# Running counts of the experts' choices: sums of neighbours and of pairs in fixed tiles, in place of a row of additions

## The chip, the cores and the metric

The kernel runs on one core of a Trainium2 chip. A core has five engines that run side by side and wait for each other through semaphores: TensorE (PE, matrix products; its weight loads are shown apart as PEld), VectorE (DVE), ScalarE (ACT), GpSimd (POOL) and SyncE (SP, which here only issues DMAs). The metric is the device time of one execution in microseconds (us), the median over several runs. The kernel before takes 1328.57 us (three runs, 1328.46 to 1329.15).

## The reference

The input x holds 8192 tokens of 512 numbers. Each token is normalized (layernorm), and the output is x plus two terms of the normalized tokens: a random-feature attention (exponentials of projections, times a matrix of weights) and a mixture of 64 experts with a shared expert beside them. The part that the change touches is the routing of the mixture:

```python
scores = sigmoid(tokens @ router_w)              # 8192 x 64
# the 4 best of 8 groups of experts are kept, and of these the 8 best experts
topk_w, topk_idx = top_k(masked_scores, 8)
flat_e = topk_idx.reshape(-1)
onehot = one_hot(flat_e, 64)
prior = cumsum(onehot, axis=0) - onehot          # choices of that expert by earlier tokens
pos = take_along_axis(prior, flat_e[:, None], axis=1)[:, 0]
valid = pos < 256                                # an expert takes its first 256 choices
```

So every expert serves the first 256 tokens that chose it, and the kernel needs, for every expert, the running count of choices over the tokens.

## The kernel before

**Stages.** The tokens are worked on in 16 blocks of 512. A block is four chunks of 128 tokens; inside a tile the 128 partitions are the tokens of a chunk, and the four chunks (index s, NS = 4) lie side by side in the columns. Until about 395 us the kernel runs a loop over the even blocks (function `dense`: shared expert `ps_gu`, features `ps_f`, the sums `ps_o`), and `routing` steps a generator `look_up(b)` for every block, even and odd, between the steps of `dense`. From there on it finds the chosen tokens of each expert (`seek`, gathers on POOL's queue), and runs the 64 experts (`hidden`, `down`), with the attention of the odd blocks laid between them (`late_attention`), and the shared expert of the odd blocks at the end (`ends`).

**One block in `look_up`.** PE transposes the normalized tokens (`ps_x`, line 356; from block 5 on they come as the copy `xc`, which POOL's queue makes by a DMA, line 339), ACT and DVE split each of the four results into a high part (line 99) and a low part `xT_l` (line 102). PE forms the logits `ps_l` (line 398), ACT copies them to `lt`, PE turns them back (`ps_lt`, line 415), and DVE works out the penalty of the groups (lines 431 to 448), the eight best of each chunk (`max`, `match_replace`, lines 459 and 460) and from these `mask_r` (line 462): 1 where a token chose an expert. `mask_r` has 128 partitions and 4 x 64 columns.

**The running sums.** `prior_r[:, s, :]` shall hold, for each partition, how often earlier chunks chose each expert. It starts with a copy of `taken`, the total of all earlier blocks (line 467). Three additions of 64 columns follow, each of which needs the one before it (line 469), and a fourth makes the new `taken` (line 472). PE then adds over the partitions: the product `both`/`ps_bu` of `prior_r` with a matrix of ones (line 479), and four small products of `mask_r` with a triangle and of `prior_r` with ones (line 490). ACT copies one half to `cu` and SP stores it (`upto`, lines 498 and 499); DVE adds from the other half to `begun` (line 518). After the last block, `chunks` turns `begun` into the lines that POOL gathers (lines 753 to 756).

**What sets the order.** The program is written in an order of yields, and a scheduler places each engine's instructions by their priorities and by an estimate of when operands are ready; `behind(a, b)` adds an edge that keeps a after b on an engine. In the code such edges hold the counting product behind the last product of the dense stream (line 486). Each engine then runs its own list strictly in order.

**Pools.** `ps_sm` holds two banks of PSUM, used in turn for two of the four transposes of a block, for `ps_l`, `ps_lt` and `ps_bu`. In the odd blocks `ps_bu` takes the bank of the second transpose, and `ps_l` of the following block that of the fourth: each is free when its `xT_l` is done. `rt` holds `mask_r`, `prior_r` and `j` once each; `act` has four slots of 2 KiB with the tag "t"; `const` is allocated for the whole run.

Of the kernel before, what the change touches and what calls it, by code (L numbers as in the profile page):

```python
# [9 lines left out]
FP = mybir.dt.float32  # L10
FPR = mybir.dt.float32r
I32 = mybir.dt.int32
AF = mybir.ActivationFunctionType
ALU = mybir.AluOpType
# [4 lines left out]
P = 128  # L19
# [3 lines left out]
E = 64  # L23
# [10 lines left out]
NS = TB // P  # L34
# [14 lines left out]
TAKEN = -3.0e38  # L49
# [5 lines left out]
def rfs_attention_moe_kernel(  # L55
# [15 lines left out]
    nc = tc.nc  # L71
    xf = x.flatten_outer_dims()

    const = ctx.enter_context(tc.tile_pool(name="const", bufs=1))
# [7 lines left out]
    rt = ctx.enter_context(tc.tile_pool(name="rt", bufs=1))  # L82
    act = ctx.enter_context(tc.tile_pool(name="act", bufs=4))
# [159 lines left out]
    nc.gpsimd.iota(erow_i, pattern=[[1, E]], base=-E, channel_multiplier=0)  # L243
    erow = const.tile([P, E], FP, name="erow")
    nc.gpsimd.tensor_copy(erow, erow_i)
    taken = const.tile([P, E], FP, name="taken")
    nc.vector.memset(taken, 0.0)

    begun = [const.tile([P, NS, E], FP, name=f"begun{h}") for h in range(NH)]
    for t in begun:  # L250
# [126 lines left out]
    def look_up(b):  # L377
# [78 lines left out]
        mr = gt_t  # L456
        top = rt.tile([P, NS, K], FP, tag="top", name="top", bufs=2)
        for s in range(NS):
            nc.vector.max(top[:, s, :], ml[:, s, :])
            nc.vector.match_replace(mr[:, s, :], top[:, s, :], ml[:, s, :], TAKEN)  # L460
        mask_r = rt.tile([P, NS, E], FPR, tag="mask", name="mask_r")
        nc.vector.tensor_scalar(mask_r, mr, TAKEN * 0.9, None, ALU.is_le)
        mask = mask_r.bitcast(FP)

        prior_r = rt.tile([P, NS, E], FPR, tag="prior", name="prior_r")
        prior = prior_r.bitcast(FP)
        nc.vector.tensor_copy(prior_r[:, 0, :], taken)
        for s in range(1, NS):
            nc.vector.tensor_tensor(
                prior_r[:, s, :], prior[:, s - 1, :], mask[:, s - 1, :], ALU.add  # L470
            )
        nc.vector.tensor_tensor(taken, prior[:, NS - 1, :], mask[:, NS - 1, :], ALU.add)
        yield
        yield

# [190 lines left out]
    for rc in range(RC):  # L666
        pool, tag = ((ps_sm, "sm"), (ps_tr, "tr"))[rc // 2]
# [52 lines left out]
    normed[0] = normalize(0, *scale0)  # L720
    split0 = last["split"]
    late = look_up(0)
    next(late)
    upper0 = last["upper"]
# [25 lines left out]
    def chunks():  # L750

        for h in range(NH):
            j = rt.tile([P, E], FP, tag="j", name="j")
            nc.vector.tensor_reduce(j, begun[h].rearrange("p s e -> p e s"), AX.X, ALU.add)
            nc.vector.scalar_tensor_tensor(line[:, :, h], j, float(E), erow, ALU.mult, ALU.add)
            nc.vector.tensor_scalar(first_of[:, :, h], j, float(P), -float(P), ALU.mult, ALU.add)
# [28 lines left out]
    def seek():  # L785

        chunks()
        ats = {}
        for e in range(E + TE):
            n, k = divmod(e, TE)  # L790
            if e < E:
                if k == 0:
                    ats[n] = kib4([P, TE, NH, P], "at", FP)
                find(ats[n], e)
            if k == 1 and n:
                tokens_of(n - 1, ats.pop(n - 1), last["dve"])
            yield
# [114 lines left out]
    def routing(t):  # L912

        for b in sorted(fronts):
            if next(fronts[b], fronts) is fronts:
                del fronts[b]
        b, k = divmod(t + GAP, GAP)
        if k == (b == 1) and b < NB:
            fronts[b] = look_up(b)
            next(fronts[b])  # L920
        if k == GAP - 3 and b + 1 < NB:
            normed[b + 1] = normalize(b + 1, *roots(b + 1, statistics(xbs[b + 1])))
        if k == 1 and b + 2 < NB:
            xbs[b + 2] = load_tokens(b + 2)
# [144 lines left out]
```

## Time and profile before

| what | value |
|---|---|
| median of the timed runs | 1328.57 us (1328.46 to 1329.15) |
| the profiled execution, its own time | 1306.77 us |
| its span, first to last instruction | 1304.9 us |
| granted TensorE clock | 1.00 |
| PE idle in the first 400 us | 4.56 us, of which 2.49 us before 40 us |
| PE idle between 400 and 1200 us | 0.56 us |
| PE idle after 1200 us | 5.55 us |

The profile takes one execution, and it is 1.9 us longer than its span; the timed runs are 21.8 us longer than the profiled one. Busy times of an engine are summed over its instructions where they don't overlap. Matmuls are pipelined: a matmul's record is longer than the distance to the next one's start (here 0.39 us against 0.226 us for 512 columns), and so the waits of PE are read from the starts. The same holds of DVE: the record of an addition over 64 columns has 0.22 us, and the next instruction starts 0.13 us after it.

### The profile page before, as it was taken

To read this page: it belongs to the slowest core of one execution; us is meant where nothing else is said; L and a number is where in the kernel's file an instruction comes from. 1 tells how busy PE (TensorE), PEld (TensorE's weight loads), DVE (VectorE), ACT (ScalarE), POOL (GpSimd) and SP (SyncE) were. 2 spreads that over 40 slices of the span, in tenths; PEclk is the share of its full clock that TensorE was granted. 3 is DMA by queue.
4 is the path that set the end of the run, shared out by engine and by line. 5 is a ranking of instruction groups with operands and counts; after the bars stand their busy time and mean duration, and the time that the engine had idled before them with its cause. 6 is when DMAs were issued, how large, how long until landed. Compare 5 with 4: busy or idle time off the path is not lost.

```text
span 1304.9 us, 21429 instructions
## 1 busy us (share of the span) xinstructions
PE 1294.3 (99%) x7670; PEld 1136.6 (87%) x7670; DVE 922.3 (71%) x1911; ACT 646.6 (50%) x1025; POOL 587.3 (45%) x690
## 2 busy tenths in 40 slices
PE   9999999999999999999999999999999999999998
PEld 7888888888888989999999999999999999988886
DVE  6978867867865776777767677777776776643555
ACT  5744444453432655566566465665665665540111
POOL 3122122113107666777677767667667654310000
PEclk9999999999999999999999999999999999999999
DMA  8665675676586989999999999999999999784995
GB/s 271 227 234 199 243 281 213 219 282 235 190 297 190 320 221 334 251 292 285 299 283 261 272 284 276 256 316 279 283 261 296 283 257 249 195 245 166 317 320 193
DMA packets 189530, 338.61 MB, mean 259 GB/s; under 512 B 15984, under 2 KB 87664, under 8 KB 189424
## 3 DMA queue, kind: packets, MB, share of 16 engines
q1 hardware_dynamic: 153488, 245.93, 54.7%
q0 software_dynamic: 35936, 91.32, 29.7%
q8 instruction: 60, 0.98, 0.3%
q14 instruction: 46, 0.38, 0.1%
HBM read 220.66 MB, written 104.99 MB: 250 GB/s over the span
## 4 chain that ended last, share of the span: by engine, by line
PE 85%; DVE 8%; DMA 2%; ACT 2%; issue 1%; SPq 1%; POOL 1%; ACTq 0%; DVEq 0%; POOLq 0%
PE ps_gu L109 41%; PE ps_e L109 13%; PE ps_o L109 10%; PE ps_y L109 6%; PE ps_fu L109 5%; PE ps_t L832 3%; PE ps_f L109 3%; PE ps_l L398 2%; DMA xb<-in_L_attn_x_dram 1%; DVE f L527 1%; PE ps_x L356 1%; DVE xT_l L102 1%; DVE st L300 1%; SPq L287 1%; POOL at L762 1%
## 5 line engine op out<-in xcount | busy, mean ns | idle before, releaser
L890 POOL DMA_INDIRECT out_dram<-ye,who x128 | 229.3, 1792 | 180.5 <-ACT ye L889 120.1
L109 PE MATMUL ps_gu<-gT,gu_h 128*128 128x256 f32 x2048 | 292.3, 285 | 0.0
L109 PEld LDWEIGHTS ps_gu<-gT,gu_h 128*128 128x128 f32 x2048 | 265.2, 190 | 9.0 <-ACT gu_h L99 4.7
L762 POOL DMA_INDIRECT at<-upto,line x128 | 139.3, 1088 | 76.0 <-DMA q<-norms 37.3
L102 DVE TENSOR_TENSOR gu_l<-gu,gu_h 128x1024 fp32r<-128x1024 f32 x128 | 155.3, 1223 | 14.6 <-ACT gu_h L99 13.7
L109 PE MATMUL ps_gu<-gT,gu_l 128*128 128x256 f32 x1024 | 164.7, 283 | 0.0
L815 POOL DMA_INDIRECT xg<-xnw,who x128 | 138.8, 1084 | 40.0 <-issue 32.0
L109 PE MATMUL ps_e<-d_h,ehT 128*128 128x512 f32 x512 | 147.8, 390 | 0.0
L109 PEld LDWEIGHTS ps_gu<-gT,gu_l 128*128 128x128 f32 x1024 | 142.6, 191 | 3.4 <-DVE gu_l L102 0.6
L99 ACT CAST gu_h<-gu 128x1024 fp32r<-128x1024 f32 x128 | 132.2, 1047 | 0.0
L889 ACT ACTIVATE ye<-ps_e,we 128x512 f32<-128x512 f32 x128 | 87.6, 688 | 84.6 <-PE ps_e L109 84.3
L109 PEld LDWEIGHTS ps_e<-d_h,ehT 128*128 128x128 f32 x512 | 94.7, 188 | 18.8 <-ACT d_h L99 0.2
L271 POOL TENSOR_TENSOR a<-rstd,ve 128x4 f32<-128x4 f32 x45 | 10.9, 243 | 201.5 <-DVE rstd L262 199.0
L99 ACT CAST ehT<-sg 128x512 fp32r<-128x512 f32 x64 | 39.9, 623 | 124.5 <-DVE sg L535 113.3
L535 DVE SCALAR_TENSOR_TENSOR sg<-sg,ps_gu 128x512 f32<-128x512 f32 x64 | 44.0, 687 | 71.4 <-PE ps_gu L109 71.4
L102 DVE TENSOR_TENSOR gT<-ps_t,gT 128x512 fp32r<-128x512 f32 x128 | 82.1, 683 | 16.8 <-ACT gT L99 16.8
L102 DVE TENSOR_TENSOR d_l<-d,d_h 128x1024 fp32r<-128x1024 f32 x64 | 78.2, 1222 | 11.7 <-ACT d_h L99 11.7
L541 ACT ACTIVATE f<-f,ab 128x512 f32<-128x512 f32 x64 | 46.3, 724 | 73.4 <-DVE f L527 72.7
L109 PE MATMUL ps_o<-wT_h,fT 128*128 128x512 f32 x288 | 80.1, 391 | 0.2 <-ACT fT L99 0.2
L109 PE MATMUL ps_e<-d_l,ehT 128*128 128x512 f32 x256 | 79.2, 390 | 0.0
L109 PE MATMUL ps_o<-d_h,hT 128*128 128x512 f32 x256 | 79.0, 396 | 0.0
L533 ACT ACTIVATE sg<-ps_gu 128x512 f32<-128x512 f32 x64 | 38.3, 598 | 77.3 <-PE ps_gu L109 77.3
(181 smaller groups left out, 2523.6 us busy)
## 6 DMA issues: line engine op xcount, KB each, us to landing
gu<-in_L_ffn_gate_w_dram SPq DMA_DIRECT2D x64, 512.0 KB
gu<-in_L_ffn_up_w_dram SPq DMA_DIRECT2D x64, 512.0 KB
d<-in_L_ffn_down_w_dram SPq DMA_DIRECT2D x64, 512.0 KB
xnw<-xw SPq DMA_DIRECT2D x32, 577.0 KB
xb<-in_L_attn_x_dram SPq DMA_DIRECT2D x32, 512.0 KB
out_dram<-xb SPq DMA_DIRECT2D x32, 512.0 KB
xT_h<-turned SPq DMA_DIRECT2D x30, 512.0 KB
xT_l<-turned SPq DMA_DIRECT2D x30, 512.0 KB
```

The costliest lines, as they stand in the source:

```text
L99: return nc.scalar.copy(dst, src)
L102: return on.tensor_tensor(dst, src, hi.bitcast(FP), ALU.subtract)
L109: last["pe"] = nc.tensor.matmul(ps, w[c][a], v[c][b], start=(start and part == 0 and c == 0), stop=(stop and part == 2 and c == n - 1),)
L398: logits = nc.tensor.matmul(pl, rwp[:, kc].rearrange("p t e -> p (t e)"), v[kc], start=(n == 0 and kc == 0), stop=(n == 1 and kc == KC - 1),)
L533: last["tanh"] = nc.scalar.activation(dst, g, AF.Tanh, scale=0.5)
L535: nc.vector.scalar_tensor_tensor(dst, dst, 0.5, u, ALU.mult, ALU.mult)
L541: nc.scalar.activation(f, f, AF.Exp, scale=ab[:, rc : rc + 1])
L762: nc.gpsimd.indirect_dma_start(out=at[:, e % TE, h, :], out_offset=None, in_=upto, in_offset=bass.IndirectOffsetOnAxis(ap=line[:, e, h : h ...
L815: nc.gpsimd.indirect_dma_start(out=xgs[e][:, h, :], out_offset=None, in_=xnw, in_offset=bass.IndirectOffsetOnAxis(ap=who[:, e, h : h + 1], ...
L832: turned_s = nc.tensor.transpose(pr[:, c, ts(h, P)], xr[:, h, ts(c2 * 2 + c, P)], ident_r)
L889: nc.scalar.activation(ye[:, h, :], po, AF.Copy, scale=wes[e][:, h : h + 1])
L890: now = nc.gpsimd.indirect_dma_start(out=out, out_offset=bass.IndirectOffsetOnAxis(ap=who[:, e, h : h + 1], axis=0), in_=ye[:, h, :], in_o ...
```

## The change

The three additions in a row are replaced by two. Two tiles, `masks` and `sums`, each with five slots of 64 columns, are allocated once for the run. Slot 0 of `masks` holds what earlier blocks chose (the old `taken`), slots 1 to 4 the masks of the four chunks. The first addition puts the sum of each slot and its left neighbour into `sums[1..4]` (256 columns). The second adds to `sums[2..3]` the pair sum two places to the left, `sums[0..1]` (128 columns), where `sums[0]` is a copy of slot 0 of `masks`. So `sums[0..3]` hold the sums up to each chunk. A third addition, of 64 columns, makes the total `sums[4] + sums[2]` in slot 0 of `masks` for the next block. The copy stands ahead of the mask in the text. The tile `j` of `chunks` moves from the pool `rt`, where it had one slot, to the four slots of `act`.

```diff
-    taken = const.tile([P, E], FP, name="taken")
-    nc.vector.memset(taken, 0.0)
+    masks = const.tile([P, 1 + NS, E], FPR, name="masks")
+    sums = const.tile([P, 1 + NS, E], FPR, name="sums")
+    masks_fp, sums_fp = masks.bitcast(FP), sums.bitcast(FP)
+    nc.vector.memset(masks_fp[:, 0, :], 0.0)
...
-        mask_r = rt.tile([P, NS, E], FPR, tag="mask", name="mask_r")
-        nc.vector.tensor_scalar(mask_r, mr, TAKEN * 0.9, None, ALU.is_le)
-        mask = mask_r.bitcast(FP)
-
-        prior_r = rt.tile([P, NS, E], FPR, tag="prior", name="prior_r")
-        prior = prior_r.bitcast(FP)
-        nc.vector.tensor_copy(prior_r[:, 0, :], taken)
-        for s in range(1, NS):
-            nc.vector.tensor_tensor(
-                prior_r[:, s, :], prior[:, s - 1, :], mask[:, s - 1, :], ALU.add
-            )
-        nc.vector.tensor_tensor(taken, prior[:, NS - 1, :], mask[:, NS - 1, :], ALU.add)
+        nc.vector.tensor_copy(sums[:, 0, :], masks_fp[:, 0, :])
+        nc.vector.tensor_scalar(masks[:, 1:, :], mr, TAKEN * 0.9, None, ALU.is_le)
+        nc.vector.tensor_tensor(sums[:, 1:, :], masks_fp[:, 1:, :], masks_fp[:, :NS, :], ALU.add)
+        nc.vector.tensor_tensor(
+            sums[:, 2:NS, :], sums_fp[:, 2:NS, :], sums_fp[:, : NS - 2, :], ALU.add
+        )
+        nc.vector.tensor_tensor(masks[:, 0, :], sums_fp[:, NS, :], sums_fp[:, 2, :], ALU.add)
+        prior_r, mask_r = sums[:, :NS, :], masks[:, 1:, :]
...
-            j = rt.tile([P, E], FP, tag="j", name="j")
+            j = act.tile([P, E], FP, tag="t", name="j")
```

## The prediction

> **What bounds the kernel.** I read the busy shares first:
>
> ```profile
> PE 1294.3 (99%) x7670; PEld 1136.6 (87%) x7670; DVE 922.3 (71%) x1911; ACT 646.6 (50%) x1025; POOL 587.3 (45%) x690
> ```
>
> PE works 1294.3 of 1304.9 us at a granted clock of 1.00. A change of DVE's work can only act through PE's waits: those it removes, or adds. So next came PE's waits over the whole run, each with its sum in us, how often, and the longest:
>
> ```profile
> PE ps_bu L479 <- DVE prior_r L469: 0.9, 4, 0.3
> PE ps_x L356 <- DMA xc<-xw: 0.4, 1, 0.4
> ```
>
> The first is the place of the change: the counting product waits for the last of the three additions. Nothing on PE after 400 us waits for routing; there it is idle for 0.56 us in 800. So what can be gained is here, and I took block 7 apart in the timeline (start, duration, engine, line, operation):
>
> ```profile
> 200.08 0.29 DVE L462 TENSOR_SCALAR mask_r<-lt 128x256 fp32r<-128x256 f32 x1
> 200.28 0.69 DVE L102 TENSOR_TENSOR xT_l<-ps_x,xT_h 128x512 fp32r<-128x512 f32 x1
> 200.88 0.22 DVE L469 TENSOR_TENSOR prior_r<-prior_r,mask_r 128x64 fp32r<-128x64 f32 x1
> 201.01 0.69 DVE L102 TENSOR_TENSOR xT_l<-ps_x,xT_h 128x512 fp32r<-128x512 f32 x1
> 201.61 0.22 DVE L469 TENSOR_TENSOR prior_r<-prior_r,mask_r 128x64 fp32r<-128x64 f32 x1
> 201.74 0.69 DVE L102 TENSOR_TENSOR xT_l<-ps_x,xT_h 128x512 fp32r<-128x512 f32 x1
> 201.85 0.61 PE L109 MATMUL ps_o<-wT_h,fT 128*128 128x512 f32 x2
> 202.34 0.22 DVE L469 TENSOR_TENSOR prior_r<-prior_r,mask_r 128x64 fp32r<-128x64 f32 x1
> 202.71 0.36 PE L479 MATMUL ps_bu<-prior_r,ones_r 128*128 128x256 f32 x1 [0.24 <-DVE prior_r L469]
> 203.30 1.13 PE L398 MATMUL ps_l<-xT_h,rwp 128*128 128x512 f32 x4
> ```
>
> DVE is never idle here, and the scheduler has put a subtraction `xT_l` between each two dependent additions. The last ends at 202.56, and PE starts 0.15 later. The two products before it started at 201.85, and two take 0.45 (as from 205.17 to 205.63), so PE could have gone on at 202.30: the real loss is 0.41 us, not 0.24. Blocks 9, 11 and 13 lose 0.37, 0.42 and 0.41 in the same way, block 5 loses 0.09; together **1.70 us**. In the other eleven blocks `ps_bu` follows its predecessor without a gap.
>
> **What the change costs on DVE.** Durations by shape, up to 395 us (count, then sum and mean in ns):
>
> ```profile
> L469 DVE TENSOR_TENSOR prior_r<-prior_r,mask_r 128x64 fp32r<-128x64 f32 x48 | 10.0, 208 | 0.0
> L442 DVE TENSOR_TENSOR lt<-lt 128x256 f32<-128x256 f32 x16 | 6.7, 420 | 0.0
> ```
>
> Per block it removes three additions of 64 columns and adds one of 256 and one of 128; the fourth, the copy and the mask keep their size. Records: 64 columns 0.22, 256 columns 0.42. No row has 128 columns; it lies between these two, and the straight line gives 0.29. What counts for DVE is the distance from start to start: 0.13 for 64 columns (200.88 to 201.01), 0.34 for 256 (209.66 to 210.00, lines 437 and 438), so 0.20 for 128, between 0.13 and 0.34. Before: 3 x 0.13 = 0.39; after: 0.34 + 0.20 = 0.54. So DVE gets **0.15 us more per block**, 2.4 us over 16 blocks. The Trainium skill (Trace Analysis, "Optimizing Scalar/DVE Operations") says otherwise twice. It puts a fixed cost of about 60 ns on every DVE instruction and advises to group them where the engine is saturated: one fewer would save an estimated 16 x 0.06 = 1 us. The rows decide: the 192 columns more, at (0.34 - 0.13)/192 = 1.1 ns each, cost 0.21, more than the saved instruction. Of an engine that is not saturated but causes bubbles elsewhere, it says to break instructions up: by that, the wide additions would make PE wait longer. The row speaks against this too, because in the list above each further dependent instruction costs the 0.60 of an `xT_l` beside its own time.
>
> **When the sums are ready.** The changed program's lists, as built, keep that pattern in blocks 5 to 13: mask, `xT_l`, 256-addition, `xT_l`, 128-addition, `xT_l`, total. In block 7: mask 200.08, 256-addition 200.88 to 201.30, `xT_l` 201.22, 128-addition 201.82 to 202.11, the third `xT_l` 202.02 to 202.71. The sums are ready at 202.11 instead of 202.56, **0.45 us earlier**. With the ends for 128 columns (0.22 and 0.42) it is 0.32 to 0.52.
>
> **What PE does with it.** Were PE's list unchanged, `ps_bu` could start at max(202.30, 202.11 + 0.15) and the loss would go. But the scheduler expects the sums earlier too: in blocks 5, 7, 9, 11 and 13 of the changed program the two `ps_o` products that stood before `ps_bu` stand behind `ps_l`. So PE arrives at 201.85, 0.45 earlier, and waits until 202.26: **0.41 again**. The wait moves with the thing waited for; the gain is 0.00, between -0.13 and +0.07 per block by the ends for 128 columns, so from 0.65 lost to 0.35 won in all.
>
> **What comes late next.** Behind the third `xT_l` is the PSUM bank that the next `ps_l` takes. Now that ends at 202.71 (before 202.43) and `ps_l` would come at 202.26 + 0.59 = 202.85; with the same 0.15 it can start at 202.86. The cover of 0.72 is used up, at a cost of 0.01; each 0.1 more in the additions would cost 0.1 in five blocks. `xb` (line 582) comes 0.28 later on DVE; its bank is one of four, and PE showed no wait for any.
>
> The order of other instructions changes as well. In the odd blocks `begun` moves ahead, and a fourth `bn_stats` (0.60) comes before the seed of the inverse root (line 262), which so moves from 206.92 to about 207.7. POOL's chain, the normalization on ACT and the two DMAs `xc` follow by 0.75; the two exponentials of line 425 are also put before the second normalization, so the first DMA is 1.0 later, behind which POOL's next chain waits (its result, needed by ACT at 224.87, comes by about 222.3). The second decides:
>
> ```profile
> 215.46 0.75 POOL L339 DMA_DIRECT2D xc<-xw  x1 [0.31 <-ACT top L501]
> 221.51 1.49 PE L356 MATMUL ps_x<-ident_r,xc 128*128 128x128 f32 x16
> ```
>
> It landed 3.2 after its issue, at 218.7. At 216.2 + 3.2 = 219.4 it is still 2.1 early. Hidden. On SP the store `upto` goes ahead of one of four small stores of the norms, which are needed 20 us later; no cost. Even blocks: `ps_bu` comes 12 us after the sums; no cost. `masks` and `sums` have one copy, as the old tiles had, and the same readers. In the first two blocks the scheduler shifts single products and lets `lt` go ahead of features on ACT; the last feature was ready at 58.99 for its first use at 59.59, and DVE is 0.15 late: no cost, at worst 0.3 by a product out of its place. `j` with four slots lets both sums of `chunks` run at once; POOL's gathers start some 0.3 earlier, and nothing on PE waits for them.
>
> **Sum.** 0.00 from the moved wait, +0.05 from the banks, 0 from what is hidden: 1306.8 us in the profiled execution (before 1306.77). I add the difference, not scaled, to the median of the timed runs: 1328.57 + 0.05 = **1328.6 us**. The runs are 1.7% longer than the profile for reasons that it doesn't show; that wouldn't make a wait of 0.4 matter.
>
> **The rivals.**
> *The wait really goes.* If the sums come more than 0.4 earlier than I reckon, or PE is late for another reason, the 1.70 us are won: 1326.9. For it: PE waits for nothing else there. Against it: PE's moved products. Chance 7%; a gain beyond 0.2% would need more than all these waits, 4%.
> *The copy `xc` comes too late.* Its landings range from 3.1 to 7.2 us. With 7.2, 216.2 + 7.2 = 223.4 is 1.9 after PE's arrival; in four blocks (transposes at 174.37, 221.51, 268.61, 315.78) that is 7.6: 1336. It decides from a landing of 5.3 on. Against it: the landings of these blocks were 3.2 to 3.4. Chance 8%, for all stalls of this size.
> *Additions and banks cost more*, 0.2 in five blocks: 1329.6. This lies within the forecast's own range.
>
> **Numbers.** What can be told from no change is about 0.2%, 2.66 us. The forecast with its own range (from 0.35 won to 0.65 and 0.3 lost, the bank, and the 0.7 spread of the runs) and the won 1.70 all fall inside: same 88%, faster 4%, slower 8%. The range, 1326.6 to 1331.0, takes in the won wait and half a stall of `xc`.
>
> **What would show it.** DVE: 128 columns 0.29, 256 columns 0.42, 16 instructions fewer, busy time up by 1.3 (records) to 2.4 (starts). PE: `ps_bu` of blocks 7, 9, 11 and 13 with a wait of 0.4 after its predecessor's 0.226 and two `ps_o` products behind `ps_l`; `ps_l` directly after `ps_bu`. The second `xc` about 0.75 later, with no wait at `ps_x`. I am wrong if `ps_bu` follows without a gap, if `ps_l` or `ps_x` waits, or if anything changes after 400 us.

## The result, and the profile after

The changed kernel takes 1331.67 us (median of 22 runs, 1326.29 to 1336.02) against 1328.78 us of the kernel before (22 runs, 1323.40 to 1330.92). The ratio is 1.0024, with an interval of 1.0013 to 1.0035: **slower by 0.24%**, 2.9 us. The forecast was 1328.6, in a range of 1326.6 to 1331.0.

The profiled execution of the changed kernel took 1332.64 us, with a span of 1330.8 us and a granted clock of 0.991. That of the kernel before took 1306.77 us at 1.000. The two profiles can't be subtracted. Of the 25.9 us between their spans, about 23 arise in one stretch: from 400 to 500 us PE works on 154 products fewer in the changed kernel, and it makes up for them only by 523 us. The busy times of that stretch are these (stretch, its length, then busy us of PE, PEld, DVE, ACT and POOL with the number of instructions, granted clock, DMA share, GB/s). Of the changed kernel:

```profile
400.00:500.00 100.00, 84.00 (x477) 73.58 (x476) 53.45 (x82) 36.04 (x53) 50.86 (x46) 0.90 0.63 190
```

Of the kernel before, in the profile that the prediction read, and then in a second profile of the same kernel (e1 below):

```profile
400.00:500.00 100.00, 99.44 (x631) 88.19 (x630) 70.42 (x110) 52.56 (x78) 68.74 (x58) 1.00 0.86 261
```

```profile
400.00:500.00 100.00, 86.50 (x486) 75.45 (x485) 54.51 (x84) 38.26 (x58) 54.04 (x47) 0.90 0.67 197
```

So the kernel before has the gap too; the first profile shows an execution without it. Of 236 timed runs of the kernel before that stand beside a profile with the gap, none took less than 1314 us, so the execution of 1306.77 us is not like them; on which chip it ran is not on record. What the change did has to be read mainly before 400 us. The busy times of the whole run, of the changed kernel, confirm what was reckoned for DVE: 16 instructions fewer, 2.0 us more.

```profile
PE 1303.3 (98%) x7670; PEld 1141.6 (86%) x7670; DVE 924.3 (69%) x1895; ACT 646.4 (49%) x1025; POOL 583.6 (44%) x690
```

PE's waits over the whole run of the changed kernel (sum in us, how often, the longest; cut to the lines that are used here):

```profile
PE ps_gu L109 <- ACT gT L99: 6.5, 1, 6.5
PE ps_gu L109 <- ACT gu_h L99: 5.2, 3, 4.0
PE ps_y L109 <- ACT fU L99: 5.2, 2, 4.6
...
PE ps_x L359 <- DMA xc<-xw: 0.8, 1, 0.8
...
PE ps_bu L480 <- DVE sums L469: 0.4, 2, 0.2
```

The first and the third line belong to the gap, and of the second the 4.0. The rest of the second line lies behind the gap, nearly all of it in one wait at 1000 us, as the list from 480 us on shows:

```profile
PE ps_gu L109 <- ACT gu_h L99: 1.2, 2, 1.1
```

The same list of e1 is empty. The wait at `ps_x` for the copy `xc` has grown from 0.4 to 0.8. The wait at `ps_bu` is still there. Read from the starts, the odd blocks 5 to 13 lose 1.3 us in all here, 1.6 in e2 and 1.7 in e18; with the old sums it is 1.1 to 1.8 in five profiles (before, e1, e4, e15, e17), so neither a gain nor a loss can be told. This is block 7 of the changed kernel, in the timeline:

```profile
201.68 0.41 DVE L468 TENSOR_TENSOR sums<-masks 128x256 fp32r<-128x256 f32 x1
...
202.22 0.61 PE L109 MATMUL ps_o<-d_h,hT 128*128 128x512 f32 x2
...
202.61 0.28 DVE L469 TENSOR_TENSOR sums<-sums 128x128 fp32r<-128x128 f32 x1
...
203.04 0.35 PE L480 MATMUL ps_bu<-sums,ones_r 128*128 128x256 f32 x1 [0.20 <-DVE sums L469]
```

The 128 columns take 0.28 us, the sums end at 202.89, and PE starts 0.15 later. After the two products from 202.22 PE could have gone on at 202.67, so it loses 0.37 here, where it lost 0.41. This part went as forecast.

### The profile page after: what moved, and what is told of

It reads as the page before. It is cut to its first block, busy times and chain, and to the rows that moved or that the text cites. A ratio compares the mean times of both kernels' runs of the same rounds, so it can differ in the third digit from the quotient of the medians.

```text
span 1330.8 us, 21421 instructions
## 1 busy us (share of the span) xinstructions
PE 1303.3 (98%) x7670; PEld 1141.6 (86%) x7670; DVE 924.3 (69%) x1895; ACT 646.4 (49%) x1025; POOL 583.6 (44%) x690
## 4 chain that ended last, share of the span: by engine, by line
PE 86%; DVE 6%; another core or an unknown queue 2%; ACT 2%; DMA 2%; issue 1%; SPq 1%; POOL 0%; DVEq 0%; ACTq 0%; POOLq 0%
PE ps_gu L109 40%; PE ps_e L109 13%; PE ps_o L109 11%; PE ps_fu L109 5%; PE ps_y L109 5%; PE ps_f L109 4%; PE ps_t L833 3%; PE ps_l L401 2%; PE ps_x L359 1%; DVE f L528 1%; ACT xw L329 1%; DMA xb<-in_L_attn_x_dram 1%; DVE st L303 1%; DVE xT_l L102 1%
## 5 line engine op out<-in xcount | busy, mean ns | idle before, releaser
L891 POOL DMA_INDIRECT out_dram<-ye,who x128 | 233.6, 1825 | 200.3 <-ACT ye L890 142.2
L109 PE MATMUL ps_gu<-gT,gu_h 128*128 128x256 f32 x2048 | 295.5, 287 | 11.7 <-ACT gT L99 6.5
L109 PEld LDWEIGHTS ps_gu<-gT,gu_h 128*128 128x128 f32 x2048 | 268.0, 192 | 22.1 <-ACT gu_h L99 9.8
L763 POOL DMA_INDIRECT at<-upto,line x128 | 133.9, 1046 | 75.7 <-issue 37.2
L816 POOL DMA_INDIRECT xg<-xnw,who x128 | 134.0, 1047 | 51.3 <-issue 41.7
L102 DVE TENSOR_TENSOR d_l<-d,d_h 128x1024 fp32r<-128x1024 f32 x64 | 78.1, 1221 | 11.7 <-ACT d_h L99 10.9
```

Source lines behind the costliest of these rows:

```text
L102: return on.tensor_tensor(dst, src, hi.bitcast(FP), ALU.subtract)
L109: last["pe"] = nc.tensor.matmul(ps, w[c][a], v[c][b], start=(start and part == 0 and c == 0), stop=(stop and part == 2 and c == n - 1),)
L763: nc.gpsimd.indirect_dma_start(out=at[:, e % TE, h, :], out_offset=None, in_=upto, in_offset=bass.IndirectOffsetOnAxis(ap=line[:, e, h : h ...
L816: nc.gpsimd.indirect_dma_start(out=xgs[e][:, h, :], out_offset=None, in_=xnw, in_offset=bass.IndirectOffsetOnAxis(ap=who[:, e, h : h + 1], ...
L891: now = nc.gpsimd.indirect_dma_start(out=out, out_offset=bass.IndirectOffsetOnAxis(ap=who[:, e, h : h + 1], axis=0), in_=ye[:, h, :], in_o ...
```

## The chain that grew

The wait at `ps_x` is in block 5. Followed backwards it leads over five engines to a step 44 us earlier. First the kernel before:

```profile
84.52 0.23 DVE L507 TENSOR_SCALAR xw<-den 128x2 f32<-128x2 f32 x2
...
85.14 1.14 SPq L510 DMA_DIRECT2D xnw<-xw  x1
...
88.57 0.37 SPq L499 DMA_DIRECT2D upto<-cu  x1
...
90.62 1.52 ACT L326 ACTIVATE xw<-xb,shift,rstd 128x512 f32<-128x512 f32 x2 [0.71 <-DMA xnw<-xw]
...
94.87 0.60 ACT L99 CAST fT<-f 128x512 fp32r<-128x512 f32 x1
...
95.89 0.68 DVE L102 TENSOR_TENSOR fT<-f,fT 128x512 fp32r<-128x512 f32 x1
...
122.88 0.77 POOL L339 DMA_DIRECT2D xc<-xw  x1 [0.42 <-ACT top L501]
...
127.63 1.38 PE L356 MATMUL ps_x<-ident_r,xc 128*128 128x128 f32 x14 [0.37 <-DMA xc<-xw]
```

The same steps of the changed kernel:

```profile
84.72 0.69 DVE L535 SCALAR_TENSOR_TENSOR r<-r,ps_gu 128x512 f32<-128x512 f32 x1 [0.32 <-ACT r L534]
85.33 0.23 DVE L508 TENSOR_SCALAR xw<-den 128x2 f32<-128x2 f32 x2
...
88.46 0.37 SPq L500 DMA_DIRECT2D upto<-cu  x1
88.92 0.97 SPq L511 DMA_DIRECT2D xnw<-xw  x2
...
92.63 0.81 ACT L329 ACTIVATE xw<-xb,shift,rstd 128x512 f32<-128x512 f32 x1 [2.79 <-DMA xnw<-xw]
...
96.69 1.13 ACT L99 CAST fT<-f 128x512 fp32r<-128x512 f32 x2
...
97.33 1.29 DVE L102 TENSOR_TENSOR fT<-f,fT 128x512 fp32r<-128x512 f32 x2 [1.42 <-ACT fT L99]
...
124.04 0.77 POOL L342 DMA_DIRECT2D xc<-xw  x1 [0.43 <-ACT top L502]
...
128.22 1.40 PE L359 MATMUL ps_x<-ident_r,xc 128*128 128x128 f32 x14 [0.78 <-DMA xc<-xw]
```

With other durations on DVE's list the scheduler puts an operation of the shared expert (`r`) ahead of the step that makes the weights `xw<-den` of block 2. These are ready 0.8 later, and in SP's list the first store `xnw` of block 2 goes behind `upto`. But `upto` waits for the counting product and `cu`: the store is issued 3.8 later (4.0 when both profiles are counted from their first counting product, as in the table below). A tile of the same pool, into which ACT writes the first normalized tokens of block 4, comes free only when the store has landed, so ACT waits 2.79 instead of 0.71. ACT's list now has the first cast `fT` behind the second exponential `f`, and DVE sits idle for 1.42 waiting for it. From there DVE is full up to the seed of block 5 (line 262 before), and the lateness reaches the second copy `xc` of block 5. That copy had no cover left before the change: in the first profile it made PE wait 0.37, and in the seven other profiles with the order of before (e1, e4, e7, e8, e12, e15, e17) PE lists no wait there but still loses 0.1 to 0.2 by the starts.

## The experiments

Below, "before" is the kernel before in runs taken beside those of the experiment, on the same chip. Each time is a median, followed by its ratio to before with the 95% interval.

### What is the same kernel worth twice? (e1, e2)

e1 is the kernel before, unchanged; e2 the changed kernel.

> The kernel before, unchanged, to see the state in which its timed runs are; its one profile had a granted clock of 1.000 and 1306.8 us, its timed runs 1328.6. Theory A (late stalls: the timed runs of both kernels hold stalls of PE of some 20 us behind the first gathers, between 405 and 460 us, and the change only lengthens them): the clock of its runs is 0.991 to 0.995 as with the kernel after, and a new profile shows PE busy for 80 to 90 of the 100 us from 400 to 500, where the first showed 99.4. Theory B (the 2.9 us come from the odd blocks before 400 us, and the late part is the same in both): the profile agrees with the first one after 400 us, and its busy PE up to 400 us is 2 to 3 us less waiting than that of the kernel after.

> The kernel after, unchanged, a second profile. Theory A: stalls of PE between 405 and 460 us again, of 15 to 25 us together, but not at the same instants; ratio 1.001 to 1.004. Theory B: PE busy up to 400 us less than with the kernel before in the same call by 2 to 3 us; the same ratio.

e1 took 1329.0 us (ratio 1.0007, 0.9998 to 1.0017), e2 1330.27 (1.0007, 0.9995 to 1.0020), before 1328.62. Both profiles have the gap between 400 and 460 us, so it is no work of the change. Counted from the first counting product of each profile, those of e1 lie within 0.4 us of those of the first profile, up to the last one at 343. e2 has the wait at `ps_x` again, 1.1 us long. The ratio of one and the same changed kernel is 1.0024 in the result and 1.0007 here, and e2's time lies inside the forecast's range: single ratios on such a chip move by more than 0.1%.

### The tile `j`, and the tiles alone (e3, e4, e15, e17)

e3 gives `j` of the changed kernel a tile that is dead by then; e4 does only the move of `j` (the last lines of the change), to the kernel before. The edit of e3:

```diff
-            j = act.tile([P, E], FP, tag="t", name="j")
+            j = earlier.rearrange("p g h -> p (g h)")
```

> The kernel after with the new sums, but the two starts of the chunks again in one tile of 64 columns of their own (the dead tile of the earlier groups), so that the six instructions of the search's start stand in the order of the kernel before. Theory A in the form that the earlier start of the gathers (about 0.3 us) makes the stalls longer: the ratio comes back to 0.999 to 1.001. Theory A in the form that fewer instructions or other instants of DVE matter, and theory B: 1.001 to 1.004, as the kernel after.

> The kernel before with its chain of sums, and the starts of the chunks in slots of the larger pool, as in the kernel after. Theory A in the form of the earlier gathers: 1.001 to 1.004. Theory B, or theory A by the instructions of DVE: 0.999 to 1.001.

e3 took 1331.01 (1.0015, 1.0004 to 1.0026), e4 1329.05 (1.0011, 0.9997 to 1.0025), and e4's counting products stand within 0.2 us of e1's. e3 keeps the loss, and shows a second one: PE waits 1.1 at `ps_o` for a feature `fT`. So `j` isn't the cause. e15 keeps the new tiles and `j` but forms the sums by three additions in a row; its lists have the order of before. e17 is the same kernel on another chip.

```diff
-        nc.vector.tensor_tensor(sums[:, 1:, :], masks_fp[:, 1:, :], masks_fp[:, :NS, :], ALU.add)
-        nc.vector.tensor_tensor(
-            sums[:, 2:NS, :], sums_fp[:, 2:NS, :], sums_fp[:, : NS - 2, :], ALU.add
-        )
-        nc.vector.tensor_tensor(masks[:, 0, :], sums_fp[:, NS, :], sums_fp[:, 2, :], ALU.add)
+        for s in range(1, NS):
+            nc.vector.tensor_tensor(
+                sums[:, s, :], sums_fp[:, s - 1, :], masks_fp[:, s, :], ALU.add
+            )
+        nc.vector.tensor_tensor(masks[:, 0, :], sums_fp[:, NS - 1, :], masks_fp[:, NS, :], ALU.add)
```

> The other part of the change alone: the fixed tiles for masks and sums and the start of the chunks in the larger pool, but three additions in a row as before. Every engine keeps the order of the kernel before (but for one of the six instructions of the search's start), and the addresses in SBUF are those of the kernel after. Theory I (order is all): ps_bu of every block as with the kernel before, time 0.9993 to 1.0007. Rival K (addresses or the fixed tiles cost something, before or after 400 us): 1.001 to 1.003.

> The fixed tiles with three additions in a row, once more and beside the kernel after: its first run gave 1.0017 (1.0002 to 1.0032), although every ps_bu up to 343 us stood where the kernel before has it. If order is all: 0.9993 to 1.0010, and 0.1% or more below the kernel after in the same call. If the tiles and addresses carry the loss: 1.0010 to 1.0025, level with the kernel after.

e15 took 1328.77 (1.0017, 1.0002 to 1.0032), though its counting products stood within 0.5 us of e1's; PE lost 15.2 us in one stall of the gap. e17 fell on a chip where no execution had the gap: 1305.94 against 1306.40 (0.9994, 0.9985 to 1.0002). So the tiles cost nothing that shows there (at most 0.3 us by the interval), and on a chip with the gap a ratio of 1.0017 can come without any cause before 400 us.

### The change where the gap is absent (e18)

The changed kernel, beside e17 on the same chip.

> The kernel after, for the same call. 1.0010 to 1.0030 by both; what counts is the distance to the run with the tiles alone.

It took 1307.86 us: 1.0013 (1.0006 to 1.0019) of before, 1.46 us, and 1.92 us above e17, from which it differs by the form of the sums alone. Busy times of e17 in three stretches, PE's first:

```profile
40.00:110.00 70.00, 69.46 (x343) 57.68 (x341) 62.42 (x212) 37.64 (x72) 12.74 (x51) 1.00 0.64 226
110.00:185.00 75.00, 74.76 (x374) 62.23 (x373) 56.69 (x193) 33.80 (x64) 21.04 (x76) 1.00 0.69 251
185.00:390.00 205.00, 204.46 (x1013) 169.75 (x1011) 151.80 (x501) 87.57 (x169) 36.57 (x133) 1.00 0.68 243
```

and of e18:

```profile
40.00:110.00 70.00, 68.50 (x335) 56.44 (x335) 60.52 (x199) 37.53 (x72) 14.87 (x51) 1.00 0.64 226
110.00:185.00 75.00, 73.62 (x367) 61.02 (x366) 57.53 (x195) 32.56 (x61) 20.81 (x76) 1.00 0.65 237
185.00:390.00 205.00, 204.41 (x1013) 169.58 (x1011) 153.66 (x491) 88.27 (x170) 36.66 (x134) 1.00 0.68 244
```

PE is idle 0.96 us more in the first stretch, 1.14 more in the second, 0.05 in the third: 2.15 in all, nearly all of it before 185 us. Read from the starts it is more: the last counting product comes 346.0 us behind the first in e18, and 343.1 in e17. PE's waits in e18 between 60 us and the end name the two places:

```profile
PE ps_o L109 <- ACT fT L99: 1.2, 2, 0.9
PE ps_x L359 <- DMA xc<-xw: 1.1, 1, 1.1
PE ps_bu L480 <- DVE sums L469: 0.7, 3, 0.3
```

In e17 the `ps_o` wait has 0.2 and there is none at `ps_x`. The new wait at `ps_o` has the same root: in e18 the second store `xnw` lands late as well, ACT waits for it 1.12 more and makes both casts `fT` only then; DVE is idle 2.37 instead of 1.42, and the feature that PE needs at 105.7 comes at 106.7.

### Which step of the chain carries it? (e5 to e7, e9 to e11, e13, e14)

The edge `behind(a, b)` keeps a after b on one engine. The first theory was the seed of block 4, which DVE does later in the changed kernel. e5 puts it back by one edge, e6 puts a `bn_stats` of block 5 back as well, e7 makes the seed late in the kernel before:

```diff
-            normed[b + 1] = normalize(b + 1, *roots(b + 1, statistics(xbs[b + 1])))
+            scale = roots(b + 1, statistics(xbs[b + 1]))
+            if b + 1 == 4:
+                behind(last["turned"], last["seed"])
+            normed[b + 1] = normalize(b + 1, *scale)
...
```

> The kernel after with one instruction of DVE moved back by an edge for the scheduler: the second instruction of the inverse root's seed for block 4 stands again ahead of the four subtractions xT_l of the next block, nothing else moves on any engine. In the first profiles of the kernel after it started 39.9 us behind the first ps_bu, in those of before 33.8, and ps_bu of block 3 was 0.5 to 1.6 us later than before. Theory C (the late seed delays POOL's root, ACT's normalization and behind it fT, for which PE waits in block 2's products): ps_bu of block 3 comes back to 63.5 to 63.6 behind the first ps_bu (after: 64.05 to 65.15), and the time falls by 0.5 to 1 us against the kernel after. Theory D (the loss lies in the longer additions themselves, or in the run alone): ps_bu of block 3 stays at 64.0 or later.

> As the run before, and besides the second bn_stats of block 5 is put ahead of the second xT_l of block 4 (in the kernel after it came behind the masks, some 10 us later than with the chain of additions). Theory C': this makes the second xc copy of block 5 issue at about 77.0 behind the first ps_bu as with the kernel before (after: 78.3 to 79.3), PE's wait of 0.7 to 1.1 us at ps_x goes down to 0.0 to 0.4, ps_bu of block 4 comes to 87.9 to 88.3 (after: 89.1 to 90.0), and the time to within 0.1% of the kernel before. Theory D: ps_x still waits 0.7 or more.

> The kernel before, chain of additions and all, with the one instruction moved the other way: the second seed instruction of block 4 stands behind the four xT_l. Theory C: ps_bu of block 3 goes from 63.5 to 64.0 to 65 behind the first one, with the wait at ps_o for fT or the late ps_x after it, and the time rises by 0.5 to 1.5 us. Theory D: no change, ps_bu of block 3 at 63.5.

e5 took 1331.27 (1.0015, 1.0002 to 1.0029), with 0.8 us at `ps_x`; e6 1330.88 (1.0019, 1.0007 to 1.0030), with 1.1; e7 1328.07 (1.0006, 0.9990 to 1.0021), with nothing changed before 400 us. So the seed isn't the cause. The next theory was the store. e9 keeps the first `xnw` of block 2 ahead of `upto` in the changed kernel; e10 puts both stores behind it in the kernel before; e11 is e9 and e6 together:

```diff
-        nc.sync.dma_start(upto[ts(b, NS * E), :].rearrange("(q p) t -> p q t", p=P), cu)
+        found = nc.sync.dma_start(upto[ts(b, NS * E), :].rearrange("(q p) t -> p q t", p=P), cu)
...
-            nc.sync.dma_start(
+            stored = nc.sync.dma_start(
...
+            if b == 2 and k == 0:
+                behind(found, stored)
```

> The kernel after with one DMA of SP's queue back where the kernel before has it: the first store xnw of block 2 ahead of the store upto, which waits for ps_bu (in the profiles of after it is issued at 43.2 behind the first ps_bu, before at 39.3, since xw<-den of DVE comes 1.0 later and the scheduler then put upto first). PE, DVE and POOL keep the order of the kernel after. Theory G: ACT's first normalization of block 4 waits for this store to free its tile; with it the first xw of block 4 comes back from 46.5 to 46.9 to about 44.7, the products and xc of block 5 issue 0.3 to 1.4 earlier (second issue 77.0 to 78.0 in place of 78.3 to 79.3) and PE's wait at ps_x falls to 0.0 to 0.7. Rival H (it is the order of DVE alone): xw comes earlier, but the second xc still issues at 78.2 or later and ps_x waits 0.7 or more.

> The mirror: the kernel before with its chain of additions, and both stores xnw of block 2 put behind upto by edges for SP's queue. The scheduler then also moves the second bn_stats of block 5 and four of ACT's instructions as in the kernel after. Theory G: the first xw of block 4 goes from 44.6 to 46.5 or later, the second xc of block 5 from 77.0 to 78 or later, PE waits 0.6 to 1.1 at ps_x, ps_bu of block 6 goes from 134.8 to 135.8 to 136.5, and the time rises by 1 to 2 us (1.0005 to 1.002). Rival H: xw late, but no wait at ps_x, ps_bu of block 6 at 134.8 to 135.1.

> The kernel after with the three instructions back: the store, the seed of block 4 and the second bn_stats of block 5. Theory G: ps_bu of block 6 at 134.6 to 135.2 behind the first (before 134.8, after 136.1 to 137.4), and a time within 0.1% of the kernel before, as the new sums themselves cost nothing on PE's path. Rival H or a rest that lies in the additions: ps_bu of block 6 at 135.8 or later, and a time 0.1 to 0.25% above.

e9 took 1330.84 (1.0018, 1.0008 to 1.0027), e10 1329.25 (1.0007, 0.9996 to 1.0019), e11 1330.6 (1.0013, 1.0001 to 1.0025). In e9 the normalization is back, but the wait at `ps_x` has 0.9; e11 still has 1.1. In both, DVE still sits idle for ACT's first cast, here in e9:

```profile
97.88 1.29 DVE L102 TENSOR_TENSOR fT<-f,fT 128x512 fp32r<-128x512 f32 x2 [1.36 <-ACT fT L99]
```

e13 is e9 with that cast put back ahead of the second exponential, and e14 is e11 with it:

```diff
-        nc.scalar.activation(f, f, AF.Exp, scale=ab[:, rc : rc + 1])
-        upper(fT[0][rc], f)
+        grown = nc.scalar.activation(f, f, AF.Exp, scale=ab[:, rc : rc + 1])
+        if last.pop("cast", None) is not None:
+            behind(grown, last["cast0"])
+        last["cast0"] = upper(fT[0][rc], f)
...
```

> The kernel after with two things back: the store xnw of block 2 ahead of upto on SP, and on ACT the first cast fT of block 2 ahead of the second exponential f of that block (in the run with the store alone DVE stood idle from 50.1 to 51.6 behind the first ps_bu, waiting for this cast, and was full from there to beyond the seed of block 5). Theory I (this idle time of DVE is what makes the second xc late): the seed of block 5 comes to 68.9 to 69.3 (70.1), the second xc is issued at 77.0 to 77.4 (78.3), ps_x waits 0.0 to 0.5 (0.8 to 1.1), ps_bu of block 6 comes to 134.8 to 135.5 (136.1 to 136.6). Rival J (the new sums themselves, or the bn_stats behind them, fill DVE): the seed stays at 69.7 or later, ps_x waits 0.6 or more.

> The same with the seed of block 4 and the second bn_stats of block 5 back as well. Theory I: as above, ps_bu of block 6 at 134.7 to 135.2, that of block 15 at 342.5 to 343.4 (before 343.0 to 343.2, after 344.3 to 344.9), time within 0.1% of the kernel before. Rival J: ps_bu of block 6 at 135.8 or later.

In e13 the first cast is ahead of the second exponential again:

```profile
95.22 0.61 ACT L99 CAST fT<-f 128x512 fp32r<-128x512 f32 x1
96.36 0.73 ACT L544 ACTIVATE f<-f,ab 128x512 f32<-128x512 f32 x1 [0.54 <-DVE f L530]
```

The wait at `ps_x` is gone from the lists of both. All 16 transposes of block 5 run in one piece, here in e13:

```profile
126.51 1.07 PE L109 MATMUL ps_gu<-xT_h,gu_l 128*128 128x512 f32 x4
127.42 1.68 PE L359 MATMUL ps_x<-ident_r,xc 128*128 128x128 f32 x16
```

The steps of the chain, in us behind the start of the first counting product of each profile (differences of start times in the timelines). The fifth row is the time from the issue of the second copy to the third transpose of block 5, the first one that reads it; the last row is PE's listed wait, where 0 stands for one of under 0.2:

| step | before | e1 | e17 | changed | e18 | e9 | e10 | e13 |
|---|---|---|---|---|---|---|---|---|
| SP issues the first `xnw` of block 2 | 39.0 | 39.0 | 39.0 | 43.0 | 43.0 | 39.6 | 42.9 | 39.6 |
| ACT begins to normalize block 4 | 44.5 | 44.4 | 44.2 | 46.7 | 46.4 | 44.5 | 46.4 | 44.5 |
| DVE begins the first `fT` of block 2 | 49.7 | 49.8 | 49.8 | 51.4 | 52.3 | 51.3 | 50.5 | 49.9 |
| POOL issues the second `xc` of block 5 | 76.7 | 76.8 | 76.9 | 78.1 | 79.3 | 78.1 | 77.2 | 77.7 |
| from there to the third transpose | 4.8 | 4.3 | 4.3 | 4.2 | 4.2 | 4.2 | 4.3 | 3.6 |
| PE waits for it | 0.4 | 0 | 0 | 0.8 | 1.1 | 0.9 | 0.4 | 0 |

The store alone (e9) mends the second row, but the third and the fourth stay as in the changed kernel; store and cast (e13) mend the second and the third, and the copy is issued 0.4 sooner than in the changed kernel, still 1.0 later than before. That it comes in time there is owed in part to its landing: 3.6 us behind its issue in e13 and e14, 4.2 in the changed kernel. With 4.2, e13 would lose some 0.6 more (an estimate). Why it landed sooner isn't shown. e10 shows the other direction: with the late store (and a `bn_stats` and four instructions of ACT that the scheduler moved with it) the kernel before begins `fT` 0.7 later (49.75 and 50.47 unrounded) and issues the copy 0.5 later, and PE waits 0.4 where e1 and e17 list no wait. So in the changed kernel the store put back alone does nothing for `ps_x`, and the cast put back with it does; the late store by itself costs something in the kernel before, and in e18 and e3, where it holds up both casts. The cast alone was not tried.

The times of e13 and e14 don't show the gain: 1329.53 (1.0021, 1.0003 to 1.0038) and 1329.92 (1.0025, 1.0014 to 1.0035), against 1327.11; e15, with the order of before, took 1328.77 beside them. Both fell on a chip with the gap, where PE lost 15.9 us in one stall of e14's profile. On the PE path before 400 us a part of the recovery is seen (the last counting product lies at 343.8 in both, at 344.3 and 344.9 in the changed kernel and e2, and at 343.2 to 343.4 in e1 and before), with 0.4 to 0.7 us left; in the time it is not shown. Neither was tried on a chip without the gap.

### What stands in the gap? (e8, e12, e16)

POOL's gathers of tokens start in the gap. e8 starts the first eight after 12 of the 16 searches in the kernel before, e12 after 8; e16 is e14 with e8's edit, which is this one:

```diff
+                        if k == 2:
+                            for e in range(4):
+                                gather(e)
...
-                    for e in range(4):
-                        gather(e)
```

> The kernel before with POOL's first four experts' gathers of tokens put ahead of the last four of the first sixteen searches, so that POOL must pause for the tokens after twelve searches; all other engines keep their order (one store of SP changes place). It asks what the 20 us of stalls from 405 to 460 us, which the usual runs of both kernels have, hang on: there DVE and ACT start up to 8 us after the product that they read has ended. Theory E (PE's signals are held while POOL issues one search after another without a pause): the pause lets them through, the stalls are shorter by 5 us or more, ratio 0.985 to 0.996. Theory F (the stalls do not depend on POOL's order): ratio 0.999 to 1.002.

> The kernel before with the tokens of the first four experts worked out, and their gathers issued, right after the first eight searches in place of sixteen (POOL: 8 searches, 8 gathers, 14 searches). The run before of this kind, after twelve searches, gave 0.9961. Theory E (PE's signals come late as long as POOL issues searches without a pause; the pause lets them through): the stalls between 400 and 460 us shrink further, ratio 0.985 to 0.995. Theory E' (what helped was only that the first gathers came earlier): also faster, 0.990 to 0.996, and stalls of the same number that begin later. Theory F (no bond): ratio 0.999 to 1.002.

> The kernel with the full order back, and POOL's first gathers after twelve searches, as in the run that gave 0.9961 on the kernel before. If the two gains and losses add up: 0.9955 to 0.9968 against the kernel before, faster than both kernels. If the place of the stalls matters more than what is in front of them: 0.997 to 1.001.

e8 took 1324.49 against 1328.12 (0.9961, 0.9948 to 0.9974), e16 1323.07 against 1327.11 (0.9970, 0.9958 to 0.9983), both faster than the kernel before. The profile of e8, of the slowest of its six executions (1327.52), has many short stalls of PE there, nine with 8.4 us in all. e12 took 1331.24 (1.0019, 1.0007 to 1.0031) with one stall of 17.5 us. So the place of the gathers moves the gap, but not in the way the theory had it, that sooner is better. Whether the gain of e8 stays where there is no gap wasn't tried.

## Why the prediction was wrong

- **"The wait moves with the thing waited for"**: right. In block 7 PE loses 0.37, forecast 0.41. The addition of 128 columns has 0.28 in block 7 (0.29 forecast) and 0.26 on average, that of 256 columns 0.41 to 0.43 (0.42); DVE's busy time rose by 2.0 us (1.3 to 2.4); `ps_l` follows `ps_bu` by 0.58 (0.59), so the bank cost nothing that can be seen. The fixed 60 ns per instruction, which the prediction takes from the Trainium skill (Perfetto Trace Analysis, "Optimizing Scalar/DVE Operations"), doesn't stand against its rows as it says: 0.13 us less 64 x 1.1 ns leaves 0.06. The 192 columns more just cost more than that.
- **"The order of other instructions changes as well"**: here is the failed step, the term "0 from what is hidden" of the sum. The prediction looked at one odd block, 7, and found 2.1 us of cover for the second `xc` that follows it (that of block 9, needed at 221.51). It didn't ask the same for block 5, whose copy has no cover; its line `ps_x <- xc 0.4` stood in the list of waits that the prediction quotes, and wasn't followed. The term, put at 0.0, is a wait of 0.7 to 1.1 us at `ps_x` in all eight profiles of the changed sums that leave the order of ACT as the scheduler made it (the result, e2, e3, e5, e6, e9, e11, e18), where seven of the eight with the order of before list none and one lists 0.4.
- **"On SP the store `upto` goes ahead of one of four small stores"** and **"Even blocks: … no cost"**: looked at the wrong stores. It was the `xnw` of the even block 2 that went behind `upto`, with 3.8 us. With the exchange of cast and exponential on ACT in the same block, which the prediction doesn't mention, this leads to the `ps_x` wait and, in e18 and e3, to about 1 us more at `ps_o`.
- **"In the first two blocks … no cost, at worst 0.3"**: the distance from the first counting product to the second grew by 0.1 us with one product of 0.23 us fewer between them, so the upper end is about what happened.
- **The rival "The copy `xc` comes too late"** (1336, 8%) had the mechanism, with the wrong place and size: four blocks with 7.6 us from late landings, where one block with a late issue cost about 1. The landings that it quotes as 3.2 to 3.4 go up to 3.9 in those blocks, and that of block 5 took 4.7. "I am wrong if … `ps_x` waits" was the right test.
- **"I am wrong if … anything changes after 400 us"**: the changed kernel waits 1.2 us behind the gap (`ps_gu` for `gu_h`). So do e2, e3, e5, e6 and e11 with 0.7 to 1.3 in all, but e13 and e18 don't, and e8, which has the old sums, loses 2.0. So the new sums alone don't make this wait, and its cause is open.
- **"The runs are 1.7% longer than the profile for reasons that it doesn't show; that wouldn't make a wait of 0.4 matter"**: true for the mean, but the profile lacked a gap whose length varies. PE's 500 products behind the last counting product take 82 to 83 us in the profiles without it (before, e17, e18). With it they take 101.3 to 104.7 in those that have the order of before (e1, e4, e7, e15), one execution each: a spread of 3.4 us, where the forecast's range is 4.4 wide.

How much of the 2.9 us is the change? Where the gap is absent it costs 1.46 us (0.8 to 2.5 by the interval), within the forecast's range. Where it is present, the result's own profile has its last counting product 0.9 to 1.1 us later than before and e1 (e2 1.5 to 1.7), and waits 1.2 more behind the gap; what the gap adds or takes away can't be told from one execution. On those chips the four kernels with the order of before (e1, e4, e7, e15) have ratios of 1.0010 on average, the seven with a wait of 0.7 to 1.1 at `ps_x` (the result, e2, e3, e5, e6, e9, e11) 1.0016, but e13 and e14, without it, 1.0023. The changed kernel itself was timed three times, at 1.0024, 1.0007 and 1.0013, and only the first time lies outside the range, by 0.7 us. So the wait that was missed is real, about 1 us; that the first time fell just above the range, and not within it as the repeat did, may be chance. The rest of the 2.9 us stays open.

## What to carry to other kernels

Where a scheduler orders the lists, a change of 0.15 us on one engine can exchange neighbours on any queue; compare all lists over all stages, and look first at waits that the profile shows already, since nothing covers what is added to them. A small DMA that is put behind one with a wait of its own takes over that wait, and so does whoever needs its buffer. And before a profile is taken for the kernel, hold its own time and clock beside those of the timed runs; if they differ, take a second profile.

## What was not expected of the hardware

The gap between 400 and 460 us holds stalls that the instructions don't explain. In e1, a timeline of PE and DVE ("remote" means that no instruction of this core was found that ended the wait):

```profile
404.19 1.07 PE L109 MATMUL ps_fu<-xT_h,pT_l 128*128 128x512 f32 x4
...
406.91 1.07 PE L109 MATMUL ps_fu<-xT_h,pT_l 128*128 128x512 f32 x4
...
418.60 0.79 PE L109 MATMUL ps_y<-wT_h,fU 128*128 128x512 f32 x1 [5.23 <-ACT fU L99]
```

```profile
410.67 0.75 DVE L527 SCALAR_TENSOR_TENSOR f<-q,ab,ps_fu 128x512 f32<-128x512 f32 x1 [1.91 <-remote]
...
416.39 0.75 DVE L527 SCALAR_TENSOR_TENSOR f<-q,ab,ps_fu 128x512 f32<-128x512 f32 x1 [3.85 <-remote]
```

The two products end at 405.26 and 407.98, and DVE reads them 5.4 and 8.4 us later, idle before it for 1.91 and 3.85; PE then waits 5.23 for what DVE and ACT make of it. In the first profile, without the gap, DVE reads the same two products 4.0 and 3.1 us after their ends, and without idle time:

```profile
409.23 0.74 DVE L527 SCALAR_TENSOR_TENSOR f<-q,ab,ps_fu 128x512 f32<-128x512 f32 x1
...
411.02 0.74 DVE L527 SCALAR_TENSOR_TENSOR f<-q,ab,ps_fu 128x512 f32<-128x512 f32 x1
```

The granted clock is 1.00 up to 410 us, 0.74 to 0.77 between 420 and 450, and 1.00 again from 460. Part of the loss is the clock's: four products of `ps_y` that take 1.09 us in the first profile take 1.91 in e1 at 419.19. In the experiments the gap was in every profile from four chips and in neither of the two from a fifth (median of before 1306.40 there, 1327.11 to 1328.62 on the four). Its cause is open.
